# A two-layer relational graph network on one core: free buffers for layer 1's last block, layer 2 begun behind its first products, the last three norms joined, the list of unseen edges in smaller pieces

## The chip, the core and the metric

The kernel runs on one core of a Trainium2 chip. A core has five engines with a queue each: PE (TensorE, matrix products into PSUM), DVE (VectorE), ACT (ScalarE), POOL (GpSimd) and SP (SyncE, which here only issues DMAs). Each works through its own queue in order; semaphores tie the queues together. Sixteen DMA engines carry the transfers. The metric is the device time of one launch in microseconds (us); the time of a kernel is the median of its runs.

## The reference

Two layers of a relational graph convolution over 12500 nodes of 128 features and 200000 edges, then a residual and a layer norm. An edge's relation is the argmax of ten of its 42 attributes. The edges are sorted by target node (`dst`); the sources are random.

```
def _rgcn_layer(x, src, dst, edge_type, w_rel, root, bias):
    seg = dst * NUM_REL + edge_type
    xs = x[src]
    sums = segment_sum(xs, seg, num_segments=N * NUM_REL)
    cnt = segment_sum(ones, seg, num_segments=N * NUM_REL)
    mean = (sums / maximum(cnt, 1.0)[:, None]).reshape(N, NUM_REL, -1)
    return einsum('nrd,rdo->no', mean, w_rel) + x @ root + bias

h = relu(_rgcn_layer(x, src, dst, edge_type, w_rel1, root1, b1))
x = layernorm(x + _rgcn_layer(h, src, dst, edge_type, w_rel2, root2, b2))
```

## The kernel before

**Edges in tiles.** 128 edges make a tile (1563 of them). For a tile POOL gathers 128 rows by an indirect DMA (`gathered`, L837), DVE builds a one-hot matrix with the edges' weights from their targets (`hots`, L844), and PE multiplies rows by one-hot, which gives the sums of a short window of nodes. DVE adds that window into an accumulator in SBUF at an offset that it loads into a register.

**Layer 1** walks all tiles in order of target (L1086, sums at L870). When all edges of a block of nodes are in, `finish` makes the block: ten products with the relations' weights, the root's, bias and ReLU. `projected_rows` and `projected_kept` then multiply the block by all ten of layer 2's relation weights and store the products in DRAM as the table YD, in three groups of columns: PE to PSUM (L938), ACT to one of two staging buffers `ys` (L944), SP to DRAM (L946). For late tiles layer 1 gathers the features of a source that is finished together with the input's row, and so does part of layer 2's sums in passing; those sums go to DRAM as SD. Six gather buffers exist (`gathers`); from tile NX on layer 1 uses four of them (`near`) and leaves two (`spare`) to layer 2.

**Layer 2** gathers rows of YD. Its loop goes over bunches p of up to four tiles. First come 45 plain bunches: 11 tiles whose sources are bounded, so that their gathers may start before YD is whole, and then the early tiles. After them come the edges that layer 1 had not yet seen with a finished source. These 678 tiles, gathered one by one as bunches of 1, 2 or 4, need a list that is put together on the chip while the plain bunches run. A pass of the loop, in program order: one-hots of bunch p+3; starts of blocks that are due (`begun`: root product from rows of hT, L1517, ACT adds the bias at L1518 and SP loads the next hT rows, L1511, one of three buffers ahead); four gathers and four products of bunch p (L1627); a piece of work from `jobs`; the sums of bunch p-2 (L1657); norms of blocks that are complete (`finish`: transposes L1559, `normed` L777 to L787, store and next load L702). With three PSUM banks, the products of bunch p wait for the sums of bunch p-3. Between single products `between` may put other PE work; so far only `seen`, the products of layer 1's stored sums (L1533, L1540), uses it. The gathered rows lie in the two spare buffers, in four groups of four tiles, filled in turn and in alternating direction.

**The list.** `brought_together` is a job, a generator whose `yield 1` hands back until four tiles further on. It loads source, count and key of the edges (L1205), marks the unseen ones, counts them with products of triangles (L1241), shifts them together in eleven steps (L1277 to L1289, large DVE passes over 127 x 1416), and cleans the result (L1296 to L1302). `put` then spreads one chunk of up to 128 tiles: DVE makes a one-hot, PE sums m products of 128x256 in PSUM (L1324), ACT copies the chunk to `packed` (L1325). The six chunks have m = 12, 9, 7, 11, 4 and 10. `listed` turns a chunk into indices (L1348 to L1417); its first part stands right behind the second chunk's `put`.

The order on each engine is the order in which the program is written out; no scheduler moves anything in this part.

Of the kernel before, what the change touches and what calls it, by code (L numbers as in the profile page):

```python
# [20 lines left out]
P = 128  # L21
# [8 lines left out]
QB = 4  # L30
# [11 lines left out]
YB = 512  # L42
# [4 lines left out]
BN = 2 * P  # L47
KSEEN = (3, 43)
KGAP = 44
HB = 4  # L50
# [20 lines left out]
def rgcn_resnorm_kernel(ctx: ExitStack, tc: tile.TileContext, x, src, dst, attr, w_rel1, root1, b1,  # L71
# [7 lines left out]
    nc = tc.nc  # L79
    N, C = x.shape  # L80
# [163 lines left out]
    def next_of(kind, of):  # L244

        turn_of_[kind] += 1
        return of[(turn_of_[kind] - 1) % len(of)]
# [662 lines left out]
    def layer_1():  # L910
# [6 lines left out]
        def finish(k, t):  # L917
# [21 lines left out]
                unkept.append(lambda: projected_kept(yb, b, h, r))  # L939

            def projected_kept(yb, b, h, r):
                ys = next_of("ys", staged)
                m = min(HB, NREL - r) * C
                nc.scalar.activation(ys[:h, :m], yb[:h, :m], AF.Copy)  # L944
                n0 = block(k)[0] + 1 + b * P
                nc.sync.dma_start(by_node[n0:n0 + h, r * C:r * C + m], ys[:h, :m])  # L946
                if (b, r) == groups[-1][::2]:
                    fin_a.pop(k)
# [233 lines left out]

    edge = STEP * (T0 + RT * SPLIT)

    def brought_together(ready, first):

        EW = P + ER
        spans_ = {}
# [105 lines left out]
        for a, b, t in ((0, KW, gl[:, :KW]), (KW, EW, go)):  # L1294
            q = t.bitcast(F32)
            nc.vector.tensor_scalar(t, d0[:, a:b], LOW - 1, None, op0=ALU.bitwise_and)  # L1296
            nc.vector.tensor_scalar(q, t, -1.0, high[:NR], op0=ALU.mult, op1=ALU.add)
            nc.vector.scalar_tensor_tensor(v[:, a:b], d0[:, a:b], 0.5, q, op0=ALU.is_gt, op1=ALU.mult)
        ga = go.bitcast(F32)
        nc.scalar.activation(ga, A[:, KW:], AF.Copy)  # L1300
        nc.vector.scalar_tensor_tensor(A[:, :KW], d0[:, :KW], 0.5, A[:, :KW], op0=ALU.is_gt, op1=ALU.mult)
        nc.vector.scalar_tensor_tensor(A[:, KW:], d0[:, KW:], 0.5, ga, op0=ALU.is_gt, op1=ALU.mult)  # L1302
        yield 1
        n = -(-NT2 // P)
# [4 lines left out]
        def put(i, c):  # L1309

            u0, u1 = c * P, min(NT2, c * P + P) - 1
            p = u1 + 1 - u0
            m = max(-(-(P - 1 + cap_of[r]) // P) for r in range(rows_at(u0, extent[u0 >= UX])[0], rows_at(u1, extent[u1 >= UX])[1] + 1))
            assert m * P <= EW
            o = i * (EW // P)
            assert o + EW // P <= EW - KW
            qc = mask[:, o:o + EW // P].bitcast(F32)
            nc.vector.tensor_scalar(qc[:NR, :m], columns[:NR, :m], f[:NR, 3:4], -float(u0), op0=ALU.add, op1=ALU.add)
            hot = hots[i % 2]
            nc.vector.tensor_tensor(hot[:, :m], columns[:NR, None, :].to_broadcast([NR, m, P]),  # L1320
                                    qc[:NR, :m, None].to_broadcast([NR, m, P]), op=ALU.is_equal)
            pp = ps_f.tile([P, YB], F32, name="pf")
            for j in range(m):
                nc.tensor.matmul(pp[:p, :2 * P], hot[:, j, :p], both[:, :, j * P:(j + 1) * P], start=(j == 0), stop=(j == m - 1))  # L1324
            nc.scalar.activation(packed[:p, c], pp[:p, :2 * P], AF.Copy)  # L1325

        put(0, first[0])
        yield 1
# [99 lines left out]
    def layer_2():  # L1428
# [84 lines left out]
        def begun(j):  # L1513
            k = begin[j]
            n0, n, _ = block(k)
            po = ps_f.tile([P, YB], F32, name="pf")
            nc.tensor.matmul(po[:, :n], rsb[1], fTs.pop(k)[:, :n], start=True, stop=True)  # L1517
            nc.scalar.activation(acc2[:, n0:n0 + n], po[:, :n], AF.Identity, bias=bsb[1])  # L1518
            features_in_turn(j + 3)
# [33 lines left out]
        def finish(j):  # L1553
# [6 lines left out]
            normed(k, xbs.pop(k), pr, (next_of("v", vs), next_of("o", os_)))  # L1560
            rows_in_turn(j + 3)

        rowP = comp.tile([1, 2 * CT], I32, name="rowP")
        for c in range(2):
            nc.sync.dma_start(rowP[:, c * CT:(c + 1) * CT], b_i[c:c + 1, :])
# [16 lines left out]
        jobs.job(0, brought_together(ready, wanted), QB)  # L1582
        made = i = ended = begins = 0
        opened = None
        for p in range(-AH, NB + BE):
# [13 lines left out]
                ohs[p + AH] = hots(keys[:, t0:t0 + n], weights[:, t0:t0 + n], columns, n, w)  # L1599
            if p == -AH:  # L1600
                jobs.run(0)
            while begins < NB2 and due_at[begin[begins]] <= i:
                begun(begins)
                begins += 1
            if p < 0:
                continue
            if p < NB:
# [16 lines left out]
                for j in range(n):  # L1624
# [3 lines left out]
                                     start=not second or j == 0, stop=not second or j == n - 1)  # L1628
                    between.run(issued[p] + j + 1)
                i = issued[p + 1]  # L1630
            if flag is None and i >= NG - 28 * QB:
                assert not jobs.due
                flagged()
                flag = i
            elif flag is not None and not flag_value and i >= flag + 20 * QB:
                flag_value.append(flag_loaded())
# [198 lines left out]
```

## Time and profile before

| what | value |
| --- | --- |
| median of 3 runs | 3087.48 us (3087.31 to 3088.15) |
| the profiled execution | 3085.23 us |
| its span, first to last instruction | 3083.4 us |
| POOL busy | 2289.6 us (74%), 2430 instructions |
| PE busy | 2210.6 us (72%) |
| DVE busy | 1986.7 us (64%) |
| ACT busy | 511.5 us (17%) |
| layer 2's first gather | 1967.4 us after the span's start |
| layer 2's last gather | 3065.2 us after the span's start |
| mean granted clock of PE | 0.803 of full speed |

A row of the timeline has: start, duration (both us), engine, line, operation, what is written `<-` what is read, shape, count of merged instructions; in brackets the idle time of the engine before it and what ended it. "issue" stands for idle time for which the profile shows no event. An engine with a q (SPq) is that engine's queue issuing a DMA; the duration is that of the issue, not of the transfer. A row of a window has, for each engine, busy time and instructions, then the granted PE clock, the DMA engines' share and GB/s. Matrix products of 32-bit numbers show as two passes each.

### The profile page before, as it was taken

The page shows a single profiled execution, that of the slowest core. Times are in us where ns is not written, and L with a number is a line of the kernel's source. Part 1 is how long each engine was busy: PE and PEld are TensorE (multiplying, and loading weights), DVE is VectorE, ACT ScalarE, POOL GpSimd, SP SyncE. Part 2 cuts the span into 40 slices and gives each one's busy share as a digit, 9 for nine tenths or more (in the row PEclk, how much of TensorE's full clock was granted, in tenths as well). Part 3 has the DMA queues.
Part 4 walks back from the last instruction along what each step waited for, and adds up shares of the span by engine and source line. Part 5 has one row for each costly group of instructions (what it writes and reads, how often), then busy time and mean ns, then how long its engine had stood idle before and what let it go on. Part 6 is the DMA issues. An engine that isn't in the chain of part 4 may idle for free. (4 is left out here: it accounts for less than half of the span.)

```text
span 3083.4 us, 37657 instructions
## 1 busy us (share of the span) xinstructions
PE 2210.6 (72%) x10645; PEld 1677.7 (54%) x10645; DVE 1986.7 (64%) x6410; ACT 511.5 (17%) x799; POOL 2289.6 (74%) x2430
## 2 busy tenths in 40 slices
PE   2768786878786878787778788644777767677554
PEld 1546575666565666566666666544544444444443
DVE  6867688978686858586767686488764334334332
ACT  2222222222222222221222221200000000000000
POOL 7777777777777777777777777676677777777775
PEclk7778888989898989998888889855778777777555
DMA  6655656666666666666666666621355454544222
GB/s 181 198 178 169 220 183 209 199 207 198 214 189 223 193 220 191 224 188 223 187 205 203 195 191 191 193 58 52 127 171 163 157 177 148 176 139 138 66 67 58
DMA packets 345316, 529.25 MB, mean 172 GB/s; under 512 B 55520, under 2 KB 225723, under 8 KB 345100
## 3 DMA queue, kind: packets, MB, share of 16 engines
q0 software_dynamic: 99552, 249.45, 28.4%
q1 hardware_dynamic: 218105, 264.48, 25.6%
q10 hardware_dynamic: 27443, 12.82, 1.4%
q8 instruction: 89, 1.46, 0.2%
q14 instruction: 127, 1.04, 0.1%
HBM read 372.75 MB, written 160.19 MB: 173 GB/s over the span
## 5 line engine op out<-in xcount | busy, mean ns | idle before, releaser
L837 POOL DMA_INDIRECT g<-XH,idxE x1386 | 1311.4, 946 | 430.3 <-issue 359.2
L1086 PE MATMUL zp<-oh,g 128*128 128x120 f32 x5898 | 944.8, 309 | 417.8 <-DVE cc L870 206.1
L1086 PEld LDWEIGHTS zp<-oh,g 128*128 128x128 f32 x5898 | 852.8, 216 | 629.8 <-DVE cc L870 353.5
L870 DVE TENSOR_TENSOR cc<-cc,zp 128x240 f32 (+1 forms) x1563 | 605.6, 387 | 430.8 <-PE zp L1086 279.9
L837 POOL DMA_INDIRECT g<-YD,idxB x678 | 640.9, 945 | 206.6 <-issue 191.9
L844 DVE TENSOR_SCALAR oh<-bank,keyE,wE 128x120 f32<-128x120 f32 x1563 | 517.3, 392 | 0.0
L1627 PE MATMUL zy<-oh,g 128*128 128x12 f32 (+30 forms) x1168 | 284.1, 358 | 231.1 <-DMA g<-YD,idxB 144.3
L1627 PEld LDWEIGHTS zy<-oh,g 128*128 128x128 f32 x1168 | 246.0, 273 | 353.8 <-DMA g<-YD,idxB 200.5
L944 ACT ACTIVATE ys<-yb 128x512 f32<-128x512 f32 (+2 forms) x291 | 152.9, 525 | 986.9 <-PE yb L938 691.7
L938 PE MATMUL yb<-w,a 128*128 128x512 f32 (+1 forms) x576 | 303.3, 613 | 5.5 <-ACT ys L944 5.5
L1540 PE MATMUL alone<-cc,w 128*128 128x512 f32 (+1 forms) x440 | 273.6, 708 | 0.0
L830 PE MATMUL pf<-cc,w 128*128 128x256 f32 (+2 forms) x1040 | 238.7, 388 | 6.3 <-DVE cc L870 5.9
L837 POOL DMA_INDIRECT g<-YD,idxE x177 | 168.0, 949 | 83.5 <-issue 59.8
L830 PEld LDWEIGHTS pf<-cc,w 128*128 128x128 f32 x1040 | 199.4, 204 | 36.5 <-issue 4.2
L1627 PE MATMUL zq<-oh,g 128*128 128x45 f32 (+33 forms) x542 | 138.2, 363 | 107.9 <-DMA g<-YD,idxB 106.5
L1627 PEld LDWEIGHTS zq<-oh,g 128*128 128x128 f32 x542 | 115.1, 261 | 182.8 <-DMA g<-YD,idxB 134.3
L799 ACT ACTIVATE cc<-zero 128x1280 f32<-128x1280 f32 x170 | 214.6, 1262 | 0.0
L777 DVE TENSOR_TENSOR cc<-pf,x 128x256 f32<-128x256 f32 (+2 forms) x52 | 21.2, 409 | 292.6 <-PE pf L1559 292.4
L837 POOL DMA_INDIRECT g<-in_x_dram,idxE x177 | 167.7, 947 | 55.6 <-issue 33.2
L844 DVE TENSOR_SCALAR oh<-columns,keyB,wB 128x45 f32<-128x45 f32 (+35 forms) x678 | 176.1, 335 | 0.0
L1657 DVE TENSOR_TENSOR cc<-cc,zy 128x12 f32 (+24 forms) x306 | 59.0, 193 | 116.5 <-PE zy L1627 95.6
L783 ACT ACTIVATE rstd<-mv,eps 128x2 f32<-128x2 f32 (+2 forms) x52 | 15.3, 295 | 682.9 <-DVE mv L781 682.8
(265 smaller groups left out, 1570.7 us busy)
## 6 DMA issues: line engine op xcount, KB each, us to landing
cc<-SD SPq DMA_DIRECT2D x21, 2560.0 KB
SD<-cc SPq DMA_DIRECT2D x41, 1280.0 KB
YD<-ys SPq DMA_DIRECT2D x194, 256.0 KB
m<-in_edge_attr_dram SPq DMA_DIRECT2D x48, 672.0 KB
g<-XH,idxE POOLq DMA_INDIRECT x1386
YD<-ys SPq DMA_DIRECT2D x97, 128.0 KB
XH<-hb SPq DMA_DIRECT2D x44, 256.0 KB
g<-YD,idxB POOLq DMA_INDIRECT x678
```

Source lines behind the costliest of these rows:

```text
L777: nc.vector.tensor_tensor(v[:p, s], pr[:p, s], xb[:p, s], op=ALU.add)
L799: nc.scalar.activation(cc[:, l, h * H:(h + 1) * H, o:o + n], zero[:, None, :n].to_broadcast([P, H, n]), AF.Copy)
L830: nc.tensor.matmul(po[:, :n], wsb[l][:, r, :], sums[:, r], start=(r == 0), stop=(w is None and r == NREL - 1))
L837: nc.gpsimd.indirect_dma_start(out=g[:, j * C:(j + n) * C], out_offset=None, in_=table, in_offset=bass.IndirectOffsetOnAxis(ap=idx, axis=0))
L844: nc.vector.tensor_scalar(oh[:, j * m:(j + 1) * m], cols[:, :m], keys[:, j:j + 1], weights[:, j:j + 1], op0=ALU.is_equal, op1=ALU.mult)
L870: nc.vector.tensor_tensor(s, s, z, op=ALU.add)
L938: nc.tensor.matmul(yb[:h, :m], fin_a[k][:, b * P:b * P + h], wsb[1][:, r:r + m // C, :], start=True, stop=True)
L944: nc.scalar.activation(ys[:h, :m], yb[:h, :m], AF.Copy)
L1086: nc.tensor.matmul(zp[:, o + l * KW:o + (l + 1) * KW], g[:, (slot[j] + l) * C:(slot[j] + l + 1) * C], oh[:, j * KW:(j + 1) * KW], start=Tr ...
L1540: nc.tensor.matmul(po[:, :n], wsb[1][:, r, :], sds[j][:, r, :n], start=(r == 0), stop=(r == NREL - 1))
L1627: nc.tensor.matmul(zp[:, o:o + w], g[:, at * C:(at + 1) * C], oh[:, j * w:(j + 1) * w], start=not second or j == 0, stop=not second or j = ...
L1657: nc.vector.tensor_tensor(s, s, zps[q][:, j * w:(j + 1) * w], op=ALU.add)
```

## The change

Four edits. **The last block of layer 1** (k = NBLK - 1) no longer stages its three groups of projected rows in `ys`, but in three of layer 1's own gather buffers (`near`), and the second group is copied by DVE instead of ACT. **The starts of blocks** stand behind the products of the bunch, from bunch 1 on, and no longer ahead of the gathers; the first three, due at once, so come behind the products of bunches 0 and 1. **The list**: cleaning the result is spread over three passes instead of one (two more `yield 1`), and a chunk's products are cut into four parts that `spread` hands to `between`, one behind each product of the next bunch. **The end**: when all sums are in and two or three blocks are left, `finish_all` makes their norms together: transposes into one PSUM tile, one root and one reciprocal for all, the results in the row buffers `x`.

PE at the end of layer 1, before (`zp` are the last block's three projected groups, `pf` starts of blocks, `zy` bunches 0 and 1):

```order
L938 MATMUL zp2_409<-w1_391,ae_15650 128x512
L938 MATMUL zp3_410<-w1_391,ae_15650 128x512
L938 MATMUL zp0_407<-w1_391,ae_15650 128x256
L1517 MATMUL pf_15720<-cc_123,root1_393 128x256
L1517 MATMUL pf_15724<-cc_123,root1_393 128x256
L1517 MATMUL pf_15728<-cc_123,root1_393 128x256
L1627 MATMUL zy0_15678<-oh6_98,g2_88 128x12 x4
L1627 MATMUL zy1_15679<-oh0_92,g2_88 128x12 x4
```

and now:

```order
L938 MATMUL zp2_409<-w1_391,ae_15650 128x512
L938 MATMUL zp3_410<-w1_391,ae_15650 128x512
L938 MATMUL zp0_407<-w1_391,ae_15650 128x256
L1666 MATMUL zy0_15678<-oh6_98,g2_88 128x12 x4
L1666 MATMUL zy1_15679<-oh0_92,g2_88 128x12 x4
L1533 MATMUL pf_15760<-cc_123,root1_393 128x256
L1533 MATMUL pf_15764<-cc_123,root1_393 128x256
L1533 MATMUL pf_15768<-cc_123,root1_393 128x256
```

The two first bunches moved ahead of the three starts. On SP the same stores stand in the same places, now from buffers of their own:

```order
L952 DMA YD_72<-ys0_99 84x256
L952 DMA YD_72<-g4_90 128x512
L952 DMA YD_72<-g5_91 128x512
L952 DMA YD_72<-g0_86 128x256
L805 DMA SD_73<-cc_123 1280x1x128
L1603 DMA rowP_15696<-b_i_163 1x16x8 x2
L1527 DMA cc_123<-hT_70 128x256 x3
```

Before, the second to fourth row read `ys1`, `ys0` and `ys1`, so the last of them waited for the first to be done with its buffer.

PE at the first chunks of the list, before (`pf<-cc` of 128x256 are a chunk's products, `zy` a bunch's):

```order
L1627 MATMUL zy0_15678<-oh1_93,g3_89 128x12 x3
L1324 MATMUL pf_16670<-cc_123 128x256 x12
L1559 MATMUL pf_16688<-ident_113,cc_123 128x128 x2
L1627 MATMUL zy1_15679<-oh2_94,g3_89 128x12 x4
L1324 MATMUL pf_16720<-cc_123 128x256 x9
L1359 MATMUL pf_16743<-ident_113,bs_f_16732 128x128
L1375 MATMUL pf_16743<-ident_113,bB_16746 1x128
L1627 MATMUL zy2_15680<-oh3_95,g3_89 128x12
```

and now, two bunches later:

```order
L1666 MATMUL zy2_15680<-oh3_95,g2_88 128x12 x3
L1666 MATMUL zy0_15678<-oh4_96,g2_88 128x12
L1338 MATMUL pf_16750<-cc_123 128x256 x3
...
L1666 MATMUL zy0_15678<-oh4_96,g2_88 128x12
L1338 MATMUL pf_16750<-cc_123 128x256 x3
L1375 MATMUL pf_16781<-ident_113,bs_f_16770 128x128
L1391 MATMUL pf_16781<-ident_113,bB_16784 1x128
L1666 MATMUL zy1_15679<-oh5_97,g2_88 128x12
L1338 MATMUL pf_16819<-cc_123 128x256 x2
```

A chunk's twelve products stood in one piece ahead of the next bunch; now three stand behind each product of that bunch. `listed`'s transposes (`bs_f`, `bB`) keep their place behind the first chunk.

The diff, cut to its core:

```diff
             def projected_kept(yb, b, h, r):
-                ys = next_of("ys", staged)
                 m = min(HB, NREL - r) * C
-                nc.scalar.activation(ys[:h, :m], yb[:h, :m], AF.Copy)
+                if k == NBLK - 1:
+                    ys = near[r // HB].rearrange("p s c -> p (s c)") if len(near[0].shape) == 3 else near[r // HB]
+                else:
+                    ys = next_of("ys", staged)
+                if k == NBLK - 1 and r == HB:
+                    nc.vector.tensor_copy(ys[:h, :m], yb[:h, :m])
+                else:
+                    nc.scalar.activation(ys[:h, :m], yb[:h, :m], AF.Copy)
...
             nc.vector.tensor_scalar(t, d0[:, a:b], LOW - 1, None, op0=ALU.bitwise_and)
             nc.vector.tensor_scalar(q, t, -1.0, high[:NR], op0=ALU.mult, op1=ALU.add)
+            if a:
+                yield 1
             nc.vector.scalar_tensor_tensor(v[:, a:b], d0[:, a:b], 0.5, q, op0=ALU.is_gt, op1=ALU.mult)
         ga = go.bitcast(F32)
         nc.scalar.activation(ga, A[:, KW:], AF.Copy)
         nc.vector.scalar_tensor_tensor(A[:, :KW], d0[:, :KW], 0.5, A[:, :KW], op0=ALU.is_gt, op1=ALU.mult)
+        yield 1
         nc.vector.scalar_tensor_tensor(A[:, KW:], d0[:, KW:], 0.5, ga, op0=ALU.is_gt, op1=ALU.mult)
...
-            pp = ps_f.tile([P, YB], F32, name="pf")
-            for j in range(m):
-                nc.tensor.matmul(pp[:p, :2 * P], hot[:, j, :p], both[:, :, j * P:(j + 1) * P], start=(j == 0), stop=(j == m - 1))
-            nc.scalar.activation(packed[:p, c], pp[:p, :2 * P], AF.Copy)
+            held = []
+
+            def some(a, b):
+                if not a:
+                    held.append(ps_f.tile([P, YB], F32, name="pf"))
+                pp = held[0]
+                for j in range(a, b):
+                    nc.tensor.matmul(pp[:p, :2 * P], hot[:, j, :p], both[:, :, j * P:(j + 1) * P], start=(j == 0), stop=(j == m - 1))
+                if b == m:
+                    nc.scalar.activation(packed[:p, c], pp[:p, :2 * P], AF.Copy)
+            spread(m, some)
...
+        def finish_all(js):
+            ks = [finals[j] for j in js]
+            pr = ps_f.tile([P, 4, C], F32, name="pf")
+            v = every[:, FIRST - 4 * BN:FIRST - 2 * BN].rearrange("p (t c) -> p t c", c=C)
+            mv = small.tile([P, 4, 2], F32, name="mv")
+            rstd = small.tile([P, 4], F32, name="rstd")
+            for t, k in enumerate(ks):
+                n0 = block(k)[0]
+                nc.tensor.transpose(pr[:, t, :], acc2[:, n0:n0 + P], ident)
+            for t, k in enumerate(ks):
+                nc.vector.tensor_tensor(v[:, t, :], pr[:, t, :], xbs.pop(k)[:, 0, :], op=ALU.add)
+                st = small.tile([P, nc.vector.BN_STATS_DIM], F32, name="st")
+                nc.vector.bn_stats(st, v[:, t, :])
+                nc.vector.bn_aggr(mv[:, t, :], st)
+            nc.scalar.activation(rstd[:, :len(ks)], mv[:, :len(ks), 1], AF.Sqrt, bias=eps)
+            nc.vector.reciprocal(rstd[:, :len(ks)], rstd[:, :len(ks)])
+            for t, k in enumerate(ks):
+                o = next_of("x", xs)
+                nc.vector.tensor_scalar(o[:, 0, :], v[:, t, :], mv[:, t, 0:1], rstd[:, t:t + 1], op0=ALU.subtract, op1=ALU.mult)
+                nc.sync.dma_start(out[block(k)[0]:block(k)[0] + P, :], o[:, 0, :])
...
+        def spread(m, some):
+            for a in range(QB):
+                between.at(i + 1 + a, lambda _, a=a * m // QB, b=(a + 1) * m // QB: some(a, b))
+        jobs.job(0, brought_together(ready, wanted, spread), QB)
...
-            while begins < NB2 and due_at[begin[begins]] <= i:
-                begun(begins)
-                begins += 1
             if p < 0:
                 continue
             if p < NB:
...
                 i = issued[p + 1]
+            while p and begins < NB2 and due_at[begin[begins]] <= i:
+                begun(begins)
+                begins += 1
...
             summed_to = min(zps, default=min(p + 1, NB))
+            if summed_to == NB and 1 < NB2 - ended <= 3:
+                finish_all(range(ended, NB2))
+                ended = NB2
             while ended < NB2 and done_at[finals[ended]] <= summed_to and (finals[ended] in whole or finals[ended] not in heavy):
```

More of the change, by code (lines that the diff above doesn't have):

```diff
@@ L1183, in rgcn_resnorm_kernel, with brought_together @@
     edge = STEP * (T0 + RT * SPLIT)
-    def brought_together(ready, first):
+    def brought_together(ready, first, spread):
         EW = P + ER
@@ L1561, in finish @@
             rows_in_turn(j + 3)
+        def finish_all(js):
+            ks = [finals[j] for j in js]
+            assert len(ks) <= 4 and all(block(k)[1] == P and (k in whole or k not in heavy) for k in ks)
+            pr = ps_f.tile([P, 4, C], F32, name="pf")
[16 more added lines that the diff above has]
+                nc.sync.dma_start(out[block(k)[0]:block(k)[0] + P, :], o[:, 0, :])
         rowP = comp.tile([1, 2 * CT], I32, name="rowP")
@@ L1581, in layer_2 @@
         wanted = list(dict.fromkeys(c for second, t0, n, _ in bunches if second for c in (t0 // P, (t0 + n - 1) // P)))
-        jobs.job(0, brought_together(ready, wanted), QB)
+        def spread(m, some):
+            for a in range(QB):
+                between.at(i + 1 + a, lambda _, a=a * m // QB, b=(a + 1) * m // QB: some(a, b))
+        jobs.job(0, brought_together(ready, wanted, spread), QB)
         made = i = ended = begins = 0
```

## The prediction

> **What bounds the kernel now.** I read the busy shares, then the chain that ended last, then the groups of the gather line.
>
> ```profile
> span 3083.4 us, 37657 instructions
> POOL 8%; issue 5%; DMA 2%; PE 0%; DVE 0%; POOLq 0%; ACT 0%; DVEq 0%
> L837 POOL DMA_INDIRECT g<-YD,idxB x678 | 640.9, 945 | 206.6 <-issue 191.9
> ...
> L837 POOL DMA_INDIRECT g<-YD,idxE x177 | 168.0, 949 | 83.5 <-issue 59.8
> ```
>
> The last chain is POOL issuing gathers. Of layer 2's 855 gathers (177 + 678) the second kind has 206.6/678 = 0.30 us of idle before each, so a gather every 1.25 us is POOL's pace. The first 177 have 83.5 us, which is 30.4 us more than 177 x 0.30. Nothing but those 30 us and the stretch after the last gather can be won in layer 2. The timeline of POOL shows where they lie.
>
> ```profile
> 1967.44 0.94 POOL L837 DMA_INDIRECT g<-YD,idxE  x1 [0.30 <-issue]
> ...
> 1985.89 0.94 POOL L837 DMA_INDIRECT g<-YD,idxE  x1 [5.02 <-issue]
> ...
> 1994.34 0.94 POOL L837 DMA_INDIRECT g<-YD,idxE  x1 [2.50 <-PE zy L1627]
> ...
> 2006.32 1.78 POOL L837 DMA_INDIRECT g<-YD,idxE  x1 [2.30 <-PE zy L1627]
> ...
> 2023.37 0.94 POOL L837 DMA_INDIRECT g<-YD,idxE  x1 [1.53 <-PE zy L1627]
> ...
> 2115.51 0.94 POOL L837 DMA_INDIRECT g<-YD,idxE  x1 [2.31 <-PE zy L1627]
> ...
> 2146.08 0.94 POOL L837 DMA_INDIRECT g<-YD,idxE  x1 [0.94 <-PE zy L1627]
> ...
> 2156.32 0.94 POOL L837 DMA_INDIRECT g<-YD,idxE  x1 [5.54 <-PE zy L1627]
> ...
> 2169.80 0.94 POOL L837 DMA_INDIRECT g<-YD,idxE  x1 [8.80 <-issue]
> ...
> 2192.72 0.94 POOL L837 DMA_INDIRECT g<-YD,idxE  x1 [3.21 <-PE zy L1627]
> ```
>
> Less 0.30 each, they stand for 4.7, 2.2, 2.0, 1.2, 2.0, 0.6, 5.2, 8.5 and 2.9 us: 12.1 us up to 2116, and 17.3 us while the list of unseen edges is made. After 2193 there is none. A releaser of PE means that the gather's buffer was still to be multiplied: the buffers hold four groups of four, and by their reversed order gather 4g takes the place of the first gather of bunch g-3, so POOL's lead over PE is 13 gathers, 16 us.
>
> **Part 1, the last block's buffers: -2.0 us.** The twelfth gather (1985.89) is the first that reads the whole table, which the last three stores complete.
>
> ```profile
> 1978.28 2.31 PE L938 MATMUL zp<-w,ae 128*128 128x512 f32 x6
> ...
> 1982.83 0.38 ACT L944 ACTIVATE ys<-zp 128x256 f32<-128x256 f32 x1 [1.14 <-DMA YD<-ys]
> 1983.24 0.32 SPq L946 DMA_DIRECT2D YD<-ys  x1
> L1547 DVE TENSOR_TENSOR cc<-cc,alone 128x512 f32<-128x512 f32 x21 | 14.3, 680 | 10.7 <-PE alone L1540 10.7
> ```
>
> Each ACT copy waits for a store to leave one of two staging buffers. With buffers of their own the copies wait for PE alone: its three products end near 1979.2, 1980.1 and 1980.6 (2560 columns in 2.31 us). ACT copies the first until 1979.9, DVE the second in about 0.68 (the nearest DVE row of that shape) until 1980.85, ACT the third until 1981.05. SP, at 0.32 a store and in order, issues the last at 1981.25 instead of 1983.24: 2.0 earlier. The gather came 2.65 after that store, so it comes at 1983.9. All behind it on SP (the sums' store, loads of hT, source, count and key rows) and DVE's first work of layer 2, which waits for the last copy, move as much. Bounds: 0.5 if the three stores, now together, land later; 2.4 if SP gains more.
>
> **Part 2, layer 2 begun behind its first products: 0.** It lets PE start bunches 0 and 1 without the hT rows, and takes the wait at 1994.34 away.
>
> ```profile
> 2004.62 1.19 PE L1517 MATMUL pf<-cc,root 128*128 128x256 f32 x2 [2.55 <-DMA cc<-hT]
> ...
> 2017.69 1.68 DVE L1246 SCALAR_TENSOR_TENSOR cc<-cc,low,go 127x1408 f32<-127x1408 f32 x1 [10.41 <-PE go L1241]
> ```
>
> But bunch 3 still stands behind the fourth start of a block, which waits for its hT rows until 2004.6, a load behind all of SP's queue. Gather 24 (2006.32) needs bunch 3, so the 2.2 us stand again there. From there PE works without a pause up to 2017.6, DVE starts at 2017.69 and is what paces layer 2 up to 2115.51. That whole chain hangs on SP's queue and moves by part 1's 2.0, no more. Bounds: 0 to -2.2, if the hT rows came sooner.
>
> **Part 3, the list in pieces: -7.5 us.** Two more rounds of DVE, and each chunk's products (12, 9, 7, 11, 4, 10) cut in four and put behind the next bunch's four products.
>
> ```profile
> 2114.63 1.89 PE L1627 MATMUL zy<-oh,g 128*128 128x12 f32 x8 [5.84 <-DVE cc L1657]
> 2138.01 1.70 DVE L1297 TENSOR_SCALAR go<-go,high 127x1416 f32<-127x1416 int32 x1
> 2142.84 1.63 DVE L1302 SCALAR_TENSOR_TENSOR cc<-cc,go 127x1416 f32<-127x1416 int32 x1 [1.27 <-ACT go L1300]
> 2145.07 0.88 DVE L844 TENSOR_SCALAR oh<-columns,keyE,wE 128x12 f32<-128x12 f32 x4
> 2147.97 7.73 PE L1324 MATMUL pf<-cc 127*128 127x256 f32 x24 [0.88 <-issue]
> 2155.73 0.39 ACT L1325 ACTIVATE packed<-pf 128x256 f32<-128x256 f32 x1 [12.92 <-PE pf L1324]
> 2155.95 0.42 DVE L777 TENSOR_TENSOR cc<-pf,x 128x256 f32<-128x256 f32 x1 [7.10 <-PE pf L1559]
> 2157.88 0.68 DVE L787 TENSOR_SCALAR o<-cc,mv,rstd 128x128 f32<-128x128 f32 x2
> 2160.94 6.77 PE L1324 MATMUL pf<-cc 127*128 127x256 f32 x18 [4.23 <-DVE cc L1320]
> 2163.90 0.77 DVE L1657 TENSOR_TENSOR cc<-cc,zy 128x12 f32 x4 [0.57 <-issue]
> 2174.05 4.99 PE L1324 MATMUL pf<-cc 127*128 127x256 f32 x22 [0.51 <-DVE bB L1394]
> 2192.28 1.56 SPq L1533 DMA_DIRECT2D cc<-SD  x2
> 2219.94 2.05 PE L1540 MATMUL alone<-cc,w 128*128 128x512 f32 x2
> ```
>
> I count in the times of before and take the 2.0 off at the end. At 2115.51 gather 108 goes out 0.9 after bunch 24's products begin: POOL's lead is used up there in both kernels. From bunch 29 (2134.88) on: its round of DVE ends with the pass that starts at 2138.01 and 0.8 of sums, so bunch 30 begins at 2140.5; then 0.88 + 1.63 + 0.28 + 0.8, bunch 31 at 2144.0; a block's norm (2155.95 to 2158.5, 2.6, with its waits 2.9) + 0.88 + 1.63 + 0.8, bunch 32 at 2149.6; 0.88 + 2.0 of one-hots + 0.77, bunch 33 at 2153.2. Up to here the 0.6 us of 2146.08 is gone.
>
> Now PE. A list product is two passes. 24 passes took 7.73 us, 22 took 4.99: 0.23 each at full clock, so 0.46 at half, and half clock for the first 4.4 us of the 24. A bunch's own eight take 1.88 at half clock. Chunk 0 with bunch 33: 8.7 us. Only then come the copy (0.4) and DVE's first look at the chunk, which is ahead of the sums that bunch 34 waits for (copied by 2156.1, sums from 2163.9; without the norm, one-hots and waits between, 2.6 + 0.6 + 0.8): bunch 34 begins 13.2 behind bunch 33. In that pause of 4.5 us the clock falls again, so chunk 1: 7.3, ending at 20.5. At full clock chunk 2: 4.4, to 24.9; chunk 3: 6.0, to 30.9, and 0.9 for DVE; chunk 4: bunch 38 at 35.5; chunk 5 with a start and transposes 6.8, bunch 39 at 42.3; the norm, one-hots and the next list's first part set bunch 40 at 49.4.
>
> POOL asks for these at 2165.5 and every 5 us. It stands 1.8 (gather 148), 2.0 (152), 1.2 (160), 0.5 (168) and 2.5 (172), then 1.8 in two waits where single-gather bunches meet four starts of a block: 9.8 against 17.3. Bounds: 2 left over, if DVE's look at a chunk delays no sums; 17 or more, if PE stays slow.
>
> Two moves on SP cost nothing. The loads of the stored sums (2192.28) now stand behind a norm's store and start two bunches later, some 10 us; they were there 27.7 us before PE used them (2219.94). A block's start, with its load of the next hT rows, moves by one bunch's products; after 2193 POOL had no wait that it could lengthen.
>
> The clock decides half of part 3.
>
> ```profile
> 2012.00:2016.00 4.00, 4.00 (x17) 3.33 (x16) 0.00 (x0) 0.00 (x0) 2.95 (x4) 0.50 0.17 49
> 2154.00:2157.00 3.00, 2.71 (x18) 2.37 (x16) 0.98 (x4) 0.39 (x1) 0.68 (x1) 1.00 0.00 0
> 2160.00:2163.00 3.00, 2.06 (x5) 1.73 (x6) 2.79 (x10) 0.00 (x0) 0.94 (x1) 0.50 0.31 92
> 2226.00:2229.00 3.00, 3.00 (x13) 1.70 (x13) 2.82 (x16) 0.47 (x1) 2.09 (x4) 1.00 0.30 75
> ```
>
> The granted clock (third number from the end) was full at the end of chunk 0 and half again after a pause of 4.2 us. At 2012 it stayed at half though PE was busy throughout, with narrow products between wide ones; at 2226 narrow and wide alternate too, and it was full. The lists will look more like the latter (2.8 of 3.2 us wide), so I take full clock. The Trainium skill (TensorE: Matmul & The Clock Gate, Part 1: The HAM clock gate) has the clock released after about 3.4 us of sustained activity; by it chunk 0 is warm halfway, the 8.7 above. The row at 2012 does not bear it out, and by that row chunk 0 would take 12.9.
>
> **Part 4, three norms joined: -1.4 us.**
>
> ```profile
> 3072.44 0.29 DVE L777 TENSOR_TENSOR cc<-pf,x 128x128 f32<-128x128 f32 x1 [0.57 <-PE pf L1559]
> ...
> 3077.51 0.34 DVE L787 TENSOR_SCALAR o<-cc,mv,rstd 128x128 f32<-128x128 f32 x1
> 3077.88 0.33 SPq L702 DMA_DIRECT2D out_dram<-o  x1
> ```
>
> Three norms one after another take 1.8 each, with a trip to ACT in each. Joined: three times add, statistics and mean (0.76 each) from 3072.44 to 3074.8, one root and reciprocal to 3075.4, three scalings at 0.3. The last store leaves SP at 3076.5 instead of 3077.9. Bounds: 0.6 if the first add waits for all three transposes, 1.5.
>
> **Sum.** 2.0 + 7.5 + 1.4 = 10.9 us off the profiled execution's 3085.23 (span 3083.4) gives 3074.3. The median of the runs shown, 3087.48, lies 2.25 above it; on that scale **3076.6 us**.
>
> **Rivals.** (a) The pieces hide the lists nearly whole, 2 us of stall left: 3087.5 - 2.0 - 15.3 - 1.4 = 3068.8. For it: at full clock a chunk with its bunch is 4.4 to 6.0 against POOL's 5.0. Against it: the lead is used up before, and chunk 0 is slow. (b) The wait only moves by two bunches: products, copy, look, sums stay in that order, and the wait at 2169.80 outlasted its products by 2 us for no cause that I can name. 15 us of stall stay, 3082. Against it: before, PE and DVE idled for each other (4.23 and 7.10 in the rows). (c) Part 1 fails, since the stores and not the copies set the landing: 3078.6. (d) Slower: with narrow products between them the lists never reach full clock. Chunks then take 12.9, 10.2, 8.3, 12.0, 5.6 and 11.0, and with the 4.5 us pause bunch 39 begins 65 behind bunch 33, not 42: 22 more, 3099. It decides from about 53 on. The row at 2012 speaks for it, that at 2226 against.
>
> **How the numbers follow.** Forecast 0.50, (a) 0.15, (b) 0.17, (c) 0.12, (d) 0.06. The range for 8 in 10 goes from (a) to just past (b): 3068 to 3083. A measurement here tells about 0.2%, 6.2 us, from no change. Faster than 3081.3: nearly all of the forecast, (a), most of (c) and a third of (b), 0.78; within 0.2%: 0.16; slower: (d), 0.06.
>
> **What would show it.** Part 1: the twelfth gather of layer 2 near 1984, ACT's copies without a DMA before them. Part 2: no wait at gather 16, a longer one at gather 24. Part 3: four waits of 1 to 3 us between 2160 and 2205, a clock of 0.5 at the second chunk and 1.0 from the third on; waits above 20 us in sum make the kernel slower. Part 4: one activation of three columns and three stores within 1.1 us. I am wrong if POOL's first 177 gathers keep over 27 us of idle beyond 0.30 each, or lose it all.

## The result, and the profile after

| | median | runs |
| --- | --- | --- |
| before | 3087.52 us | 22 |
| the change | 3093.95 us | 22 |

The ratio is 1.0022, 95% interval 1.0015 to 1.0028: the change is 6.8 us slower (4.6 to 8.6). 3076.6 was predicted. One of the change's 22 runs was a slow one of 4255.78 us, and the ratio leaves it out.

The page of the change, the same rows as before:

```profile
span 3093.1 us, 37650 instructions
L837 POOL DMA_INDIRECT g<-YD,idxB x678 | 640.7, 945 | 206.8 <-issue 190.2
...
L837 POOL DMA_INDIRECT g<-YD,idxE x177 | 168.0, 949 | 93.7 <-issue 52.8
```

The 678 later gathers go as before (206.8 us of idle against 206.6). The first 177 have 93.7 us of idle, 10.2 more. The timeline of POOL in the change, the same places as in the prediction:

```profile
1966.20 0.94 POOL L837 DMA_INDIRECT g<-YD,idxE  x1 [0.30 <-issue]
...
1988.83 0.94 POOL L837 DMA_INDIRECT g<-YD,idxE  x1 [9.21 <-issue]
...
2009.00 1.84 POOL L837 DMA_INDIRECT g<-YD,idxE  x1 [4.26 <-PE zy L1666]
...
2171.47 0.94 POOL L837 DMA_INDIRECT g<-YD,idxE  x1 [3.67 <-PE zy L1666]
...
2181.84 0.94 POOL L837 DMA_INDIRECT g<-YD,idxE  x1 [5.69 <-PE zy L1666]
...
2191.35 0.94 POOL L837 DMA_INDIRECT g<-YD,idxE  x1 [4.83 <-PE zy L1666]
...
2221.59 0.94 POOL L837 DMA_INDIRECT g<-YD,idxE  x1 [3.08 <-PE zy L1666]
```

The two long waits of the list, at 2156.32 and 2169.80 before, are gone. In their place stand seven, every four gathers from 2171 to 2222: less 0.30 each, 3.4, 5.4, 4.5, 3.3, 1.3, 2.8 and 2.8 us, in sum 23.5 against 17.3. The wait at gather 16 is gone too, and gather 24 (2009.00) waits 4.0 instead of 2.0.

The twelfth gather waits 8.9 us instead of 4.7, but most of that isn't the change. Layer 1's last activation `ae` started at 1976.88 before and at 1980.40 in the change: 20 products of a block (L830) took 2.46 us at full clock in the one profile and 4.56 at half in the other, with the same instructions. Over the profiles below, in which that part is the same code, `ae` starts between 1974.9 and 1984.2. I therefore count from `ae`: the twelfth gather comes 9.0 us later before and 8.4 in the change.

Put together from the waits: the list +6.3, gathers 12 to 129 (8.2 us of waits before, 8.0 now) -0.2, the twelfth gather -0.6, and from the first of the last transposes to the span's end 12.6 us instead of 11.5, +1.1. In sum +6.5 (before rounding), close to the 6.8 of the ratio.

Why the list waits more can be read from PE and DVE. The timeline of the change, the first three chunks (`pf<-cc` is a chunk's product, `zy` a bunch's; L1329 makes the one-hot of the next chunk, L1699 the sums that let PE begin the next bunch):

```profile
2155.81 0.60 PE L1666 MATMUL zy<-oh,g 128*128 128x12 f32 x2 [1.51 <-DVE cc L1699]
...
2163.65 1.54 PE L1338 MATMUL pf<-cc 127*128 127x256 f32 x6
2165.23 1.35 DVE L1329 TENSOR_TENSOR cc<-columns,go 127x1152 f32<-127x1152 f32 x1 [8.54 <-PE pf L1338]
2166.50 0.22 DVE L1364 CAST li<-packed 128x128 int32<-128x128 f32 x1
...
2169.76 0.77 DVE L1699 TENSOR_TENSOR cc<-cc,zy 128x12 f32 x4 [0.57 <-issue]
2170.59 0.60 PE L1666 MATMUL zy<-oh,g 128*128 128x12 f32 x2 [0.97 <-DVE cc L1699]
...
2176.57 1.54 PE L1338 MATMUL pf<-cc 127*128 127x256 f32 x6
2178.15 1.09 DVE L1329 TENSOR_TENSOR cc<-columns,go 127x896 f32<-127x896 f32 x1 [6.69 <-PE pf L1338]
...
2180.35 0.77 DVE L1699 TENSOR_TENSOR cc<-cc,zy 128x12 f32 x4
2181.18 0.39 PE L1666 MATMUL zy<-oh,g 128*128 128x12 f32 x2 [0.58 <-DVE cc L1699]
...
2187.08 1.62 DVE L1329 TENSOR_TENSOR cc<-columns,go 127x1408 f32<-127x1408 f32 x1 [5.03 <-PE pf L1338]
...
2190.48 0.60 PE L1666 MATMUL zy<-oh,g 128*128 128x12 f32 x2 [3.44 <-DVE cc L1699]
```

PE and DVE take turns. PE works on a bunch with its chunk while DVE waits for it 8.5 us; then DVE makes the next one-hot, looks at the list and adds the sums, while PE, but for two small transposes of the list, waits 5.4 us (2165.2 to 2170.6); then PE has 7.5 and DVE waits 6.7, and PE pauses 3.1; and so on. Before, bunch and chunk stood one behind the other, and PE had the bunch to work on while DVE made the next one-hot. The same place there:

```profile
2167.75 1.09 DVE L1320 TENSOR_TENSOR cc<-columns,go 127x896 f32<-127x896 f32 x1 [2.15 <-PE pf L1324]
2167.77 0.96 PE L1627 MATMUL zy<-oh,g 128*128 128x12 f32 x8
```

What DVE waits for is odd. The one-hots have two areas, X and Y, used in turn; the next one-hot goes into the area that PE does *not* read. But a chunk's products read the edges (A) and the cleaned keys as one view with a stride, and X and Y lie between the two. My theory 1: the view's span is what holds DVE back. Theory 2 was the prediction's rival (d): the clock.

### The profile page after: what moved, and what is told of

Same layout as the page of the kernel before. It is cut to its first block, busy times and chain, and to the rows that moved or that the text cites. A ratio compares the mean times of both kernels' runs of the same rounds, so it can differ in the third digit from the quotient of the medians.

```text
span 3093.1 us, 37650 instructions
## 1 busy us (share of the span) xinstructions
PE 2204.5 (71%) x10645; PEld 1676.5 (54%) x10645; DVE 1987.3 (64%) x6409; ACT 511.0 (17%) x796; POOL 2288.2 (74%) x2430
## 4 chain that ended last, share of the span: by engine, by line
POOL 20%; PE 16%; issue 15%; DVE 14%; DMA 13%; ACT 1%; DVEq 1%; SPq 0%; POOLq 0%; ACTq 0%
POOL g L837 20%; DMA g<-XH,idxE 8%; PE zp L1092 6%; DMA g<-YD,idxB 4%; DVE cc L870 4%; DVE oh L844 3%; PE yb L938 2%; PE pf L830 2%; PE alone L1556 2%; PE pf L1338 1%; PE zy L1666 1%; DVE cc L1295 1%; DVE cc L1699 1%; DMA row<-b_r 1%; ACT cc L818 1%
## 5 line engine op out<-in xcount | busy, mean ns | idle before, releaser
L837 POOL DMA_INDIRECT g<-YD,idxB x678 | 640.7, 945 | 206.8 <-issue 190.2
L830 PE MATMUL pf<-cc,w 128*128 128x256 f32 (+2 forms) x1040 | 233.6, 382 | 7.4 <-DVE cc L870 7.0
L837 POOL DMA_INDIRECT g<-YD,idxE x177 | 168.0, 949 | 93.7 <-issue 52.8
L830 PEld LDWEIGHTS pf<-cc,w 128*128 128x128 f32 x1040 | 196.0, 201 | 35.5 <-issue 3.9
L1699 DVE TENSOR_TENSOR cc<-cc,zy 128x12 f32 (+24 forms) x306 | 59.0, 193 | 116.4 <-PE zy L1666 95.7
L938 PEld LDWEIGHTS yb<-w,a 128*128 128x128 f32 x576 | 104.1, 226 | 8.5 <-ACT ys L950 8.5
```

What stands on the lines that cost most here:

```text
L830: nc.tensor.matmul(po[:, :n], wsb[l][:, r, :], sums[:, r], start=(r == 0), stop=(w is None and r == NREL - 1))
L837: nc.gpsimd.indirect_dma_start(out=g[:, j * C:(j + n) * C], out_offset=None, in_=table, in_offset=bass.IndirectOffsetOnAxis(ap=idx, axis=0))
L938: nc.tensor.matmul(yb[:h, :m], fin_a[k][:, b * P:b * P + h], wsb[1][:, r:r + m // C, :], start=True, stop=True)
L1699: nc.vector.tensor_tensor(s, s, zps[q][:, j * w:(j + 1) * w], op=ALU.add)
```

## The experiments

Each number near 1 is the ratio to the kernel before, run alongside on the same chip, with its 95% interval; gains and losses in us are that ratio less 1, times 3087. A time beside it is the kernel's own median, where the kernel before had 3087.64 or 3085.53. The first four kernels ran on another chip; there the 678 later gathers of layer 2 go out 1.44 to 1.45 us apart in the mean, not 1.25, and the kernel before takes 3641.73.

**Which edit costs the time: the list whole again, or alone.** The first kernel is the change with `put` and the cleaning as before; the second is the kernel before with those edits alone.

```diff
-            if a:
-                yield 1
             nc.vector.scalar_tensor_tensor(v[:, a:b], d0[:, a:b], 0.5, q, op0=ALU.is_gt, op1=ALU.mult)
...
-        yield 1
         nc.vector.scalar_tensor_tensor(A[:, KW:], d0[:, KW:], 0.5, ga, op0=ALU.is_gt, op1=ALU.mult)
...
-            spread(m, some)
+            for j in range(m):
+                nc.tensor.matmul(pp[:p, :2 * P], hot[:, j, :p], both[:, :, j * P:(j + 1) * P], start=(j == 0), stop=(j == m - 1))
+            nc.scalar.activation(packed[:p, c], pp[:p, :2 * P], AF.Copy)
```

> The changed kernel with the list as it was before (a chunk's products in one piece, no extra passes); free buffers, the later starts and the joined norms stay. If the list in pieces is what costs the time, this kernel is at or slightly below the kernel before: the last stall of layer 2 ahead of 2130 us and the tail are worth -0.6 (the twelfth gather, counted from layer 1's last activation ae), 0 and +0.3 by the profiled execution of the change, in sum 3087 +- 2, and POOL's stalls behind gather 130 come to about 17 us as before. If instead the other three edits are to blame (the twelfth gather waited 8.9 us and not 4.7, and the tail was 0.9 longer), it is 3092 or more.

> The kernel before with the list in pieces alone. If the list costs the time: about 3093.5, stalls of POOL behind gather 130 of 21 to 25 us against 17.3. If the other edits do: 3085 to 3088, whatever the profile shows at the list.

On that chip: 1.0001 (0.9988 to 1.0014) with the list whole, 1.0020 (1.0006 to 1.0033) with the list in pieces alone. The list it is, though POOL's waits can't be added up there. The page's row and one wait of POOL, list whole:

```profile
L837 POOL DMA_INDIRECT g<-YD,idxB x678 | 641.5, 946 | 340.8 <-issue 181.7
...
2520.58 0.94 POOL L837 DMA_INDIRECT g<-YD,idxE  x1 [3.78 <-remote]
```

POOL's own 945 ns for a gather are the same, yet the idle time has grown from 206.6 to 340.8 us in waits of some 3 us every 16 to 20 gathers. The profile calls what ends these waits "remote": it finds no instruction of the core behind it. Why this chip is slower was not found. POOL waits there all along layer 2, so a late PE cannot be read from its waits. So both were run again.

> The changed kernel with the list as before, once more: on the chip of the first comparison each gather of layer 2 took 1.43 us and not 1.25 in the mean, so that POOL's lead was used up everywhere and waits of PE counted for less. Where gathers come each 1.25 us: if the list in pieces is what makes the change slower, -1 to -3 us against the kernel before (stalls behind gather 130 near 17); if the other edits are to blame, +4 or more.

> The kernel before with the list in pieces alone, where gathers come each 1.25 us. If the waits of POOL add up to the time: stalls behind gather 130 of 22 to 25 us against 17.3, +5 to +8 us against the kernel before; with the other three edits near zero in sum, that is the whole loss of the change (+6.4). If the loss is shared, +1 to +3.

Each gather took 1.25 us there. List whole: +1.9 us (-1.2 to +4.6), 17.1 us of waits at the list; -1 to -3 was expected, so the other edits gain 1.2 at the most. List in pieces alone: +6.5 us (+3.4 to +9.9), 21.9 us. The loss is the list's; the other three edits are near nothing.

**What DVE waits for: the areas apart.** X and Y are put ahead of A, so that A and the keys stand side by side and the view spans nothing else.

```diff
-        for name, m in (("A", EW), ("X", EW), ("Y", EW), ("K", ER), ("S", ER), ("V", ER)):
+        for name, m in (("X", EW), ("Y", EW), ("A", EW), ("K", ER), ("S", ER), ("V", ER)):
...
-        below = flat[:, EW + P:EW + P + ER // 2].bitcast(BF16)
+        below = flat[:, P:P + ER // 2].bitcast(BF16)
...
         v = flat[:NR, far:far + EW]
+        far = EW
...
         both = bass.AP(A.tensor, A.offset, [A.ap[0], [far, 2], [1, EW]])
```

> The changed kernel; in the list's buffer the two one-hot areas X and Y stand ahead of A and the cleaned keys, no longer between them, so that the view that a chunk's products read (A and the keys as one access pattern) no longer spans the one-hot areas. Theory 1: DVE's one-hot of the next chunk waits for the last product of this chunk only because of that span (it writes the other area), the sums stand behind it, and the next bunch waits for the sums; as bunch and chunk now end together, PE and DVE take turns and the clock falls in every pause. Then the waits of that one-hot for PE (8.5, 6.7 and 5.0 us at the first three) go, the clock stays full from the second or third chunk on, POOL's stalls behind gather 130 fall from 23.5 to 4 to 10, and the time to 3076 to 3081. Theory 2: narrow products between wide ones keep the clock down, whatever DVE does: stalls stay above 18, the time above 3089.

> The kernel before with the same two areas moved. Theory 1: the next chunk's one-hot waited there 2.15 and 0.62 us for the products too, with bunch and chunk one after the other, so that PE had work meanwhile: stalls behind gather 130 fall from 17.3 to 13 to 16, 3084 to 3087. Theory 2: no change, 17.3 and 3087.5.

On the slower chip: 0.9992 (0.9979 to 1.0005) for the change with the areas apart, 1.0011 (0.9999 to 1.0024) for the kernel before with them. In both traces the waits for the view were gone, but neither time can be told from that of the kernel before, and the second kernel's expectation was not settled. The first was run again:

> The changed kernel with the two one-hot areas ahead of A and the keys, once more for the same reason. Theory 1 (the one-hot's wait for the chunk before is handed on by the sums behind it): stalls behind gather 130 of 8 to 12 us against 23.5 in the change, 3078 to 3084 where the change has 3094. One such wait is left: the first piece of the index list, which stands behind the second one-hot, needs the first chunk itself. Theory 2 (narrow products between wide ones keep the clock down): 18 or more, above 3088.

-7.7 us (-10.5 to -4.9), 3079.15; waits at the list 9.5 us. The waits of the one-hot's line, of the change and then of this kernel (the idle time ahead of its six one-hots, its releaser, how often):

```profile
L1329 DVE TENSOR_TENSOR cc<-columns,go x6: 686/1420/1753, 2153.3 to 2202.9; 127x1536 f32<-127x1536 f32 x1, 127x1152 f32<-127x1152 f32 x1, 127x896 f32<-127x896 f32 x1, 127x1408 f32<-127x1408 f32 x1
...
  PE pf L1338: 24.2, 4
```

```profile
L1330 DVE TENSOR_TENSOR cc<-columns,go x6: 687/1422/1753, 2156.1 to 2192.9; 127x1536 f32<-127x1536 f32 x1, 127x1152 f32<-127x1152 f32 x1, 127x896 f32<-127x896 f32 x1, 127x1408 f32<-127x1408 f32 x1
...
  PE pf L1339: 2.9, 1
```

24.2 us in four waits have become 2.9 in one (a true one: it writes the area that the products of the chunk before last have just read). The edit moves addresses and no instruction, so it is where the areas lie that made DVE wait. That it is the view's span fits this, but one thing is left open: the fifth of the six one-hots (2191.38) did not wait in the change, nor in the kernel before (2176.62), though its area lies in the span as well. So the exact rule is not shown.

**Who hands the wait on: the sums ahead of the job.** In each pass the job now stands behind the sums of bunch p-2; first with the areas as in the change, then with both.

```diff
-            jobs.run(i)
             ...
             for q in [q for q in sorted(zps) if q <= p - (1 if p >= NB - 4 else BE)]:
...
                 del zps[q]
+            jobs.run(i)
```

> The changed kernel with the job moved behind the sums of bunch p-2 in each pass, areas as in the change. The one-hot still waits for PE, but the sums that let the next bunch begin stand ahead of it. Theory 1: PE begins the next bunch at once and waits only inside it, for the one-hot (1.4 us and its trip) and at the first chunk for the first piece of the index list: stalls of 8 to 14 us, 3080 to 3086. If the sums' place is not what hands the wait on: as the change, 23 and 3094.

> Both: areas apart and the sums ahead of the job. Theory 1: neither wait reaches PE; what is left is the half clock of the first chunk (8.7 us with its bunch against POOL's 5.0): stalls of 2 to 6 us, 3072 to 3080, faster than both kernels. Theory 2: no better than 18 us of stall.

Sums first: 0.9977 (0.9967 to 0.9986), 3078.92, 12.7 us at the list, a little faster than expected. Its one-hots still wait 16.2 us for PE, but PE waits less for DVE. Both together: 0.9959 (0.9944 to 0.9974), 3075.03, 6.1 us at the list. Waits of DVE-paced passes ahead of the list go as well: those of gathers 12 to 129 fall from 8.0 to 4.6 and 3.8, which was not expected. The clock of the two kernels, by stretches of 3 us (busy time of PE, its weights, DVE, ACT, POOL; then the granted clock), the change first:

```profile
2157.00:2160.00 3.00, 3.00 (x10) 2.46 (x9) 0.00 (x0) 0.00 (x0) 2.39 (x3) 0.50 0.24 64
...
2163.00:2166.00 3.00, 2.19 (x12) 1.60 (x10) 0.77 (x1) 0.38 (x1) 2.29 (x3) 1.00 0.17 45
...
2169.00:2172.00 3.00, 1.78 (x5) 1.34 (x6) 1.79 (x10) 0.00 (x0) 0.53 (x1) 0.50 0.00 0
...
2178.00:2181.00 3.00, 0.49 (x3) 0.29 (x2) 2.61 (x11) 0.38 (x1) 0.00 (x0) 1.00 0.00 0
...
2190.00:2193.00 3.00, 2.52 (x8) 2.17 (x9) 2.83 (x15) 0.00 (x0) 1.34 (x2) 0.50 0.00 0
```

```profile
2172.00:2175.00 3.00, 3.00 (x17) 2.47 (x16) 1.95 (x4) 0.38 (x1) 0.94 (x1) 1.00 0.08 22
...
2181.00:2184.00 3.00, 2.82 (x16) 2.39 (x15) 2.86 (x11) 0.38 (x1) 1.95 (x3) 1.00 0.15 44
...
2190.00:2193.00 3.00, 3.00 (x18) 2.69 (x17) 0.00 (x0) 0.00 (x0) 2.08 (x4) 1.00 0.15 44
```

In the change the clock rises to 1.00 at the end of a chunk, narrow products between wide ones or not, and falls again in the pause behind it or, after the second pause, 1 us behind its end. With both edits one pause of 3.1 us is left, behind the first chunk, and half clock follows it (2167 to 2171); from there to the end of the last chunk there is none, and the clock stays at 1.00. So theory 2 falls: the narrow products don't keep the clock down here, the pauses do. Why it was half throughout the row at 2012 of the prediction stays open. The Trainium skill (TensorE: Matmul & The Clock Gate, Why this matters for your kernels) warns of idle gaps of over some 3 us between bursts of products; the trace agrees, with pauses of 5.4 and 3.1 us. Behind a shorter one of the change, 2.5 us from 2202.9 on with one short product in it, half clock followed too (2207 to 2209).

**What the cutting is worth.** The same two edits, with the list whole:

> Areas apart and sums ahead of the job as in the fastest version so far (stalls of 6.1 us behind gather 130, 3075), but a chunk's products in one piece as before, without the two extra passes. If cutting the products has a worth of its own once DVE no longer waits for PE: stalls of 10 to 15 us, 3079 to 3084. If the order of the sums and the span of the view were all that mattered: 4 to 8 us and 3073 to 3077.

1.0001 (0.9992 to 1.0010), with 20.4 us of waits at the list: more than the 17.1 with the order as it was. The list in pieces is thus worth 14 us of waits (20.4 to 6.1), once DVE no longer waits for PE; neither expectation had it that large. The cut of the products and the two extra passes were not taken apart. The change cut the products and left what made the cut useless.

**The two ends.** The fastest version so far with edits one and four undone, and the same with the second of the last three stores issued by ACT.

```diff
-                nc.sync.dma_start(out[block(k)[0]:block(k)[0] + P, :], o[:, 0, :])
+                (nc.scalar if t == 1 else nc.sync).dma_start(out[block(k)[0]:block(k)[0] + P, :], o[:, 0, :])
```

> The fastest version so far with edits one and four undone: layer 1's last block through the two staging buffers, the last three norms one by one. Theory A (the profiles of seven kernels with and three without the joined norms: 12.0 to 12.6 against 11.2 to 11.5 us from the first of the last transposes to the span's end): the joined norms cost 0.8, and the tail here is 11.2 to 11.6. The free buffers gain 0.3 to 0.7: the twelfth gather of layer 2 comes 9.0 after the start of layer 1's last activation ae, not 8.3 to 8.8. In sum no measurable change of the time. Theory B (both save what was forecast, 1.4 and 2.0): tail of 13.5, 10.5 after ae, 3.4 us slower.

> The fastest version so far; of the last three stores the second is issued by ACT. With all three on SP the second store's issue took up to 1.60 us, its neighbours 0.33 and 0.37. If that is the queue, still busy with the first store's rows: three issues of under 0.7 each, the last 1.0 to 1.6 earlier after the last transposes, the tail 10.8 to 11.5 instead of 12.2. If it is the three stores landing together: the last one leaves earlier, and the span ends no earlier, 12.0 to 12.4.

Ends as before: 0.9955 (0.9941 to 0.9969), 3073.09. Store by ACT: 0.9947 (0.9933 to 0.9961), 3071.31. The times of these two and of the kernel with both edits can't be told apart; the traces can. First transpose, scalings and stores at the end, in the change:

```profile
3080.48 0.90 PE L1588 MATMUL pf<-ident,cc 128*128 128x128 f32 x3 [0.99 <-DVE cc L1699]
...
3084.27 0.86 DVE L1598 TENSOR_SCALAR x<-cc,mv,rstd 128x128 f32<-128x128 f32 x3
...
3085.07 1.60 SPq L1599 DMA_DIRECT2D out_dram<-x  x1
...
3086.77 0.37 SPq L1599 DMA_DIRECT2D out_dram<-x  x1
```

With norms one by one (ends as before):

```profile
3064.17 0.69 PE L1570 MATMUL pf<-ident,cc 128*128 128x128 f32 x2 [1.00 <-DVE cc L1689]
...
3066.45 4.00 SPq L702 DMA_DIRECT2D out_dram<-o  x3
```

With the second store on ACT:

```profile
3064.94 0.90 PE L1589 MATMUL pf<-ident,cc 128*128 128x128 f32 x3 [1.22 <-DVE cc L1695]
...
3069.37 0.37 ACTq L1600 DMA_DIRECT2D out_dram<-x  x1
3069.62 1.19 SPq L1600 DMA_DIRECT2D out_dram<-x  x1
```

From the first transpose to the span's end: 11.2 to 11.5 us in five profiles with norms one by one, 12.0 to 12.6 in eight with joined norms, 11.0 with the store on ACT (3064.94 to 3075.9). The second store that SP issues right behind another takes 0.9 to 1.6 us where one by itself takes 0.33, so the last of three leaves SP 5.6 to 6.3 us after the first transpose, against 5.9 with norms one by one. Most of the loss comes behind it: the span ends 6.0 to 6.4 us after that last store when the three stand close together, and 5.3 to 5.5 when they are 1.8 apart; why is open. With the second store on ACT (0.37), the last one leaves 1.5 earlier, and the end comes 1.3 earlier than in the version that differs in that line alone. SP's second store still took 1.19, where under 0.7 was expected. The Trainium skill (DMA: Bandwidth & Descriptors, Rules for kernel authors) has it that spreading DMAs over engines saves only time to issue; that time is what is saved here, by this one trace.

The first edit: the twelfth gather comes 8.9 to 9.0 us after `ae` in the three profiles with staging buffers, 8.3 to 8.9 in the seven with buffers of their own; on average it gains 0.4.

**All kernels on the chips with a gather each 1.25 us,** in us. Waits are those over 0.45 beyond a gather each 1.25; "by waits" is their difference to the kernel before, with that of the two ends; "measured" has its interval.

| kernel | waits 12-129 | waits at the list | `ae` to twelfth | end | by waits | measured |
| --- | --- | --- | --- | --- | --- | --- |
| before | 8.2 | 17.3 | 9.0 | 11.5 | | |
| the change | 8.0 | 23.5 | 8.4 | 12.6 | +6.5 | +6.8 (4.6, 8.6) |
| list whole | 7.1 | 17.1 | 8.4 | 12.3 | -1.1 | +1.9 (-1.2, 4.6) |
| list in pieces alone | 8.2 | 21.9 | 8.9 | 11.3 | +4.3 | +6.5 (3.4, 9.9) |
| areas apart | 7.8 | 9.5 | 8.3 | 12.0 | -8.4 | -7.7 (-10.5, -4.9) |
| sums first | 4.6 | 12.7 | 8.8 | 12.1 | -7.8 | -7.1 (-10.2, -4.3) |
| both | 3.8 | 6.1 | 8.7 | 12.2 | -15.2 | -12.7 (-17.3, -8.0) |
| both, list whole | 5.0 | 20.4 | 8.9 | 12.3 | +0.6 | +0.3 (-2.5, 3.1) |
| both, ends as before | 5.4 | 7.3 | 8.9 | 11.4 | -13.0 | -13.9 (-18.2, -9.6) |
| both, a store on ACT | 5.0 | 7.2 | 8.3 | 11.0 | -14.5 | -16.4 (-20.7, -12.0) |

POOL's waits account for every time within its interval. The fastest kernels beat both the kernel before and the change.

## Why the prediction was wrong

**The bound: right.** POOL's pace is 1.25 us a gather, and only its waits in the first 177 gathers and the ends move the time.

**Part 1 (-2.0; measured -0.4).** The change's own profile has -0.6, the mean over the profiles is -0.4. The mechanism was there: ACT's copies wait for PE alone. `ae`, the last copy of the group and the last stores, in the change:

```profile
1980.40 0.37 ACT L749 ACTIVATE ae<-pf,b 128x128 f32<-128x128 f32 x1 [3.63 <-PE pf L832]
...
1983.48 2.04 SPq L952 DMA_DIRECT2D YD<-g  x3
...
1984.15 0.38 ACT L950 ACTIVATE g<-zp 128x256 f32<-128x256 f32 x1 [0.69 <-PE zp L938]
```

Two terms of the sum were mis-sized. The last copy ends 4.1 us after the start of `ae`, as forecast, but its store left 4.8 after it, not 4.4 as the steps to 1981.25 have it. And "the gather came 2.65 after that store" did not carry over: it is 2.65 or 2.66 with staging buffers and 3.5 to 4.1 with the stores closer together. The lower bound of 0.5, the three stores landing later, was the answer; what makes them later was not tried, and stays open.

**Part 2 (0): right,** with no wait at gather 16 and a longer one at gather 24 that takes its place.

**Part 3 (-7.5; measured +6.3).** Up to bunch 33 the steps hold: predicted at 2153.2 in the times of before, it began at 2155.81 with gather 108 later by 2.64, so at 2153.2. Behind it, bunches 34 to 39 begin so many us after bunch 33:

| bunch | 34 | 35 | 36 | 37 | 38 | 39 |
| --- | --- | --- | --- | --- | --- | --- |
| predicted | 13.2 | 20.5 | 24.9 | 30.9 | 35.5 | 42.3 |
| measured | 14.8 | 25.4 | 34.7 | 43.3 | 49.5 | 57.4 |

The first is nearly right, the second already 4.9 too early: the failed steps are "chunk 1: 7.3, ending at 20.5", with the next bunch right behind it, and "At full clock chunk 2: 4.4, to 24.9". I had DVE's look at the chunk hold up the sums once, at chunk 0, and let PE run through from there. But the next one-hot waits for the last product at chunks 1 and 2 too, which is now also the last of the bunch: PE stands all but still for 5.4, 3.1 and 3.4 us behind the first three, and the next chunk runs at half clock for the most part as well. Of the 15.1 us that bunch 39 comes late, 9.0 are pauses (14.4 us in sum, with 2.5 behind the fifth chunk, where 5.4 were counted) and 6 are longer chunks, above all chunk 2 (5.9 us, not 4.4) and chunk 3 (8.6, not 6.0). The wait could be read before (2.15 us at 2167.75, shown above), and I did not ask why a write into a free area should wait.

**The rivals.** (b) had the order right, "products, copy, look, sums", and priced it at 15 us of stall, no worse than before; it missed that bunch and chunk would end together. (d) had the right side and the right point, 53 us for bunch 39, where 57 was measured, but by the wrong cause: the clock did reach full before the end of each of the first four chunks. What I took for full clock from the row at 2226 was right as such; that PE would not stand still was assumed.

**Part 4 (-1.4; measured +1.1 in the change's profile, +0.8 in the mean).** DVE did its part: the last scaling ends 4.65 us after the first transpose (3080.48 to 3085.13) where it took 5.92 (3071.93 to 3077.85). The failed step is "the last store leaves SP at 3076.5", 4.6 after the first transpose: it takes 0.3 for each store, the second took 1.60, and the last left at 6.3, where before it left at 5.9. And the sum lets the end follow the last store as before, 5.5 us behind it; it came 6.3 behind it.

## What to carry to other kernels

Where a write waits although its own area is free, look for a strided view that spans it: putting what is read together side by side costs nothing and took 24 us of waits down to 3. Interleaving a piece of work with the next item makes both end at the same time, so whoever waited for the piece now waits for both; look at what stands behind that waiter on its engine, and put what releases the next item ahead of it. An edit that fails may still be most of a gain: the list in pieces lost 6 us alone and is worth 13 with the wait gone (+0.3 to -12.7).

## What the runs showed of the hardware

At the kernel's end a store of 64 KB that SP issued right behind another took 0.9 to 1.6 us to issue, instead of 0.33. One chip was 18% slower than the others on one program (3641.73 us against 3087.64): POOL's busy time is the same (2291.1 us against 2288.8, the change with the list whole on both), while the later gathers go out each 1.44 to 1.45 us instead of 1.25. And the time of layer 1's end varied by over 9 us (1974.9 to 1984.2) between profiles of the same instructions, 2 of them by whether twenty products (L830) fell into half or full clock.
